# Three emission edits in a graph attention layer: four record loads on another queue, two norms' means emitted later

## The chip, the cores and the metric

The kernel runs on one core of a Trainium2 chip. Its time is the device time of one execution in microseconds (us). The core has five engines that run side by side, each in its own order: PE (TensorE, matrix products; PEld is its weight load), DVE (VectorE), ACT (ScalarE), POOL (GpSimd) and SP (SyncE, here a queue for transfers). An instruction that isn't ready holds up everything behind it on its engine. DMA queues belong to SP, ACT and POOL; row gathers by index are issued by POOL.

## What is computed

One layer of a graph transformer over 4096 nodes of width 512, 8 heads of 64, all in float32:

```python
hs = layer_norm(x);  ht = layer_norm(h_target)
q = (ht @ Wq + bq) / 8;  k = hs @ Wk + bk;  v = hs @ Wv + bv
logits = where(adj != 0, einsum('thd,shd->hts', q, k), -1e30)
ctx    = einsum('hts,shd->thd', softmax(logits), v)
ht     = layer_norm(ht + ctx @ Wo + bo)              # the norm called n2
ff     = gelu(ht @ W1) @ W2                          # 512 -> 2048 -> 512
out    = layernorm(x + ht + ff)                      # the norm called n3
```

`adj` holds few edges in a row (a node has some 17 neighbours, at most 39 here), so the kernel works on lists of neighbours and doesn't form the 4096 x 4096 logits. A dense fallback (`general_path`) stands behind a flag and isn't run on these inputs.

## The kernel before

**Tiles, slots and records.** The 4096 targets are sorted by their number of neighbours and cut into 32 tiles of 128. A tile has as many slots as its largest node has neighbours (11 to 39; 603 slots in all). For each tile there is a record of 29 words a row, with the row's number (`TGT`), its degree, its norm factors and its first 24 neighbours. The tiles come in two parts of 16. Part A's list is sorted first; part B's edges are found and sorted, and its records scattered to HBM (L871), while part A is already in attention. `prefetch` (L989 to L999) loads the record of tile i+2 when the first slots of tile i are requested: for part A on POOL's queue, for part B on SP's (L998). A record has six buffers.

**Attention.** `attention` (L1186) works through 211 steps of up to three slots (S = 3). For each slot POOL gathers 128 rows of 4 KB, key and value of one neighbour, from HBM into a ring of 17 to 20 slots (`gather`, L984); the requests run four or five steps ahead. In each step DVE multiplies the keys by the query (L1242) and sums them to logits (L1247), ACT takes the exponential, DVE and ACT multiply the values (L1203, L1226), DVE adds some slots (L1207), and PE adds the rest up by transposing into PSUM (`cps`, L1214). Each step yields twice to the weaver; one such yield is a half group of slots.

**The end of a tile.** `finish` (L1097) is a generator that `attention` advances once per half group. It normalizes, multiplies by Wo (L1131, L1135), copies to `h` (L1140) and measures it. When a group (one or two tiles; 17 groups) is complete, it computes the norm n2: DVE adds eps (`n_ve`, L680), POOL raises to the power -0.5 (`n_rs`, L687), DVE multiplies that by the negative mean (`n_nm`, L692), ACT applies both to `h` (L1153), and PE transposes `h` into `h2T` (L1162) for the feed-forward.

**Feed-forward.** `feed` (L1332) waits for `h2T`, then alternates W1 products (`pf`, L1347), gelu on ACT (L1350) and W2 products (`po`, L1356). Halfway it gathers the rows of `x` for the residual (`xt`, L1375). It ends with the generator `end` (L1298) for the norm n3, advanced once per block of the next group's feed-forward: sum and square, `n_ve` (L1312), `n_rs` on POOL, `n_nm` (L1317), ACT's scaling (L1320) and the scatter to the output by POOL (L1324). A buffer of `xt` is free for the next gather when that scatter has landed.

**What sets the order.** `_weave` (L400) emits attention, feed-forward and the lists of part B in turn, by costs that the generators yield; attention and feed-forward of a group have the same total cost. The framework then places the emitted instructions on the engines and may change their order on an engine where one is ready earlier by its own estimates. The engines run in the order so fixed.

Of the kernel before, what the change touches and what calls it, by code (L numbers as in the profile page):

```python
# [17 lines left out]
P = 128  # L18
# [360 lines left out]
RW = E0 + RE  # L379
# [64 lines left out]
def adj_resnorm_kernel(  # L444
# [33 lines left out]
    nc = tc.nc  # L478
# [4 lines left out]
    NT = N // P  # L483
# [29 lines left out]
    recs_d = [dram.tile([n * P, RW], I32, name=f"rec{i}") for i, (_, n) in enumerate(PARTS)]  # L513
# [19 lines left out]
    with tc.tile_pool(name="keep", bufs=1) as keep:  # L533
# [17 lines left out]
        with ExitStack() as late:  # L551
# [126 lines left out]
            def shifted(pool, mv, n, name):  # L678
                ve = pool.tile([P, n], F32, name=name + "_ve")
                nc.vector.tensor_scalar_add(ve, mv[:, :, 1], EPS)  # L680
                return ve

            def power(pool, mv, n, name, ve=None):
                if ve is None:
                    ve = shifted(pool, mv, n, name)
                rs = pool.tile([P, n], F32, name=name + "_rs")
                nc.gpsimd.tensor_tensor(rs, ve, mhalf[:, :n], ALU.pow)  # L687
                return rs

            def negmean(pool, mv, rs, n, name):  # L690
                nm = pool.tile([P, n], F32, name=name + "_nm")
                nc.vector.scalar_tensor_tensor(nm, mv[:, :, 0], -1.0, rs, op0=ALU.mult, op1=ALU.mult)  # L692
                return nm

            def stats(pool, src, mv, name):
                st = pool.tile([P, 6], F32, name=name + "_st")
                nc.vector.bn_stats(st, src)
                nc.vector.bn_aggr(mv, st)
# [290 lines left out]
            def prefetch(i):  # L989
                if i >= NT or i in recs:  # L990
                    return
                r0 = TILES[i][0]
                part = 1 if r0 >= PARTS[1][0] * P else 0
                assert part in done
                r0 -= PARTS[part][0] * P
                rec = sp.tile([P, E0 + MAXE], I32, name="rec", bufs=6)

                (nc.sync if part else nc.gpsimd).dma_start(rec[:, :RW], recs_d[part][r0:r0 + P, :])  # L998
                recs[i] = rec  # L999

            def front(i, idle=0):
# [95 lines left out]
            def finish(i, p, cps, group, hs, mv):  # L1097


                rec, tq, cap = recs[i], tqs.pop(i), TILES[i][1]  # L1100

                nc.vector.scalar_tensor_tensor(p[:, :cap, :], rec[:, E0:E0 + cap].unsqueeze(2)
                                               .to_broadcast([P, cap, H]), 0.0, p[:, :cap, :],
                                               op0=ALU.is_gt, op1=ALU.mult)
                nc.vector.tensor_reduce(sums[:, i, :], p[:, :cap, :].rearrange("p j h -> p h j"),
                                        AX.X, ALU.add)
                ri = sp.tile([P, H], F32, name="ri")
                nc.vector.tensor_scalar_max(ri, sums[:, i, :], SUM_LO)
                nc.vector.reciprocal(ri, ri)
                rx = sp.tile([P, KC, P], F32, name="rb", bufs=1)  # L1110
                rxf = rx.rearrange("p c t -> p (c t)")
                nc.scalar.copy(rxf.rearrange("p (h d) -> p h d", h=H),
                               ri.unsqueeze(2).to_broadcast([P, H, HD]))
                yield
                yield
                prx = ps.tile([P, KC, P], F32, name="t", bufs=2)
                for c in range(KC):
                    nc.tensor.transpose(prx[:, c, :], rxf[:, c * P:(c + 1) * P], ident)
                ct = sp.tile([P, KC, P], F32, name="rb", bufs=1)
                nc.scalar.copy(ct, prx)  # L1120
                yield
                yield
                nc.vector.tensor_mul(ct, cps, ct)
                yield
                yield
                yield
                yield
                pa = ps.tile([P, D], F32, name="t", bufs=2)

                for c in range(KC):  # L1130
                    nc.tensor.matmul(pa[:, c * P:(c + 1) * P], tq[:, D + c * P:D + (c + 1) * P],  # L1131
                                     ident, is_transpose=True, start=c == 0, stop=False,
                                     skip_group_check=True)
                for c in range(KC):
                    nc.tensor.matmul(pa, ct[:, c, :], wo[:, c, :], start=False,  # L1135
                                     stop=c == KC - 1, skip_group_check=True)
                turned.add(i)
                yield
                h = sp.tile([P, D], F32, name="h")
                nc.scalar.copy(h, pa)  # L1140
                yield
                stats(sp, h, mv[:, len(hs), :], "n2")
                hs.append(h)
                if len(hs) < len(group):
                    return
                nh = len(hs)
                ve = shifted(sp, mv[:, :nh, :], nh, "n2")
                yield
                rs = power(sp, mv[:, :nh, :], nh, "n2", ve)
                yield  # L1150
                nm = negmean(sp, mv[:, :nh, :], rs, nh, "n2")
                for j, h in enumerate(hs):
                    nc.scalar.activation(h, h, AF.Identity, bias=nm[:, j:j + 1], scale=rs[:, j:j + 1])  # L1153
                yield
                yield
                w = len(hs) * P
                h2T = sp.tile([P, KC, 2 * P], F32, name="h2T")
                for k2 in range(KC // 2):
                    pt = ps.tile([P, 2, 2 * P], F32, name="t", bufs=2)
                    for k in range(2):  # L1160
                        for j, h in enumerate(hs):
                            nc.tensor.transpose(pt[:, k, j * P:(j + 1) * P],  # L1162
                                                h[:, (k2 * 2 + k) * P:(k2 * 2 + k + 1) * P], ident)
                    for k in range(2):
                        kc = k2 * 2 + k
                        nc.scalar.activation(h2T[:, kc, :w], pt[:, k, :w], AF.Identity,  # L1166
                                             bias=b2c[:, kc:kc + 1], scale=s2c[:, kc:kc + 1])
                h2Ts[GROUPS.index(group)] = h2T
# [129 lines left out]
            def end(group, xs, po):  # L1298

                nt = len(group)  # L1300
                sm = sp.tile([P, 2, 2], F32, name="sm3")
                for j in range(nt):
                    nc.vector.scalar_tensor_tensor(xs[j], xs[j], 1.0, po[j], op0=ALU.mult,
                                                   op1=ALU.add, accum_out=sm[:, j, 0:1])
                nc.vector.tensor_scalar_mul(sm[:, :nt, 0], sm[:, :nt, 0], -1.0 / D)
                yield
                for j in range(nt):
                    nc.scalar.activation(po[j], xs[j], AF.Square, bias=sm[:, j, 0:1],
                                         accum_out=sm[:, j, 1:2])
                yield  # L1310
                ve = sp.tile([P, nt], F32, name="n3_ve")
                nc.vector.tensor_scalar(ve, sm[:, :nt, 1], 1.0 / D, EPS, op0=ALU.mult, op1=ALU.add)  # L1312
                yield
                rs = power(sp, None, nt, "n3", ve)
                yield
                nm = sp.tile([P, nt], F32, name="n3_nm")
                nc.vector.tensor_mul(nm, sm[:, :nt, 0], rs)  # L1317
                yield
                for j in range(nt):
                    nc.scalar.activation(xs[j], xs[j], AF.Identity, bias=nm[:, j:j + 1],  # L1320
                                         scale=rs[:, j:j + 1])
                yield
                for j, i in enumerate(group):
                    ins = nc.gpsimd.indirect_dma_start(  # L1324
                        out=out[:, :], out_offset=bass.IndirectOffsetOnAxis(
                            ap=tags[:, i, TGT:TGT + 1], axis=0),
                        in_=xs[j], in_offset=None)

                    tc.declare_no_dep(ins.ins, group="out", reason="other rows")
                    tc.add_to_no_dep_group("out", ins.ins)  # L1330

            def feed(g):  # L1332
# [55 lines left out]
                output(*last)  # L1388
                yield cost
                ends.append(end(group, xs, po))  # L1390
                if g + 1 == len(GROUPS):
                    while ends:
# [124 lines left out]
```

## Time and profile before

| | |
|---|---|
| median of three runs | 1804.25 us (1801.67 to 1813.1) |
| the profiled execution's own time | 1802.71 us |
| its span in the profile | 1800.9 us |
| attention starts, last gather of keys | about 282 us, about 1640 us |
| last scatter to the output | 1783.1 us |
| granted PE clock, mean | 0.964 |

A row of a group or a wait names engine, line and operation, and reads `out<-in`: what is written from what. In the list of waits, `PE cps L1214 <- DVE kv L1207` means that PE stood idle before an instruction of L1214 until an instruction of L1207 on DVE had ended; the numbers are the total, the count and the longest. `issue` is time in which the engine waited for nothing that the profile shows. In a timeline, a row has its start, its duration, the engine and the instruction, and in brackets the idle time before it with what ended it. A row of stretches has its start and end, then for each engine busy time and, in parentheses, the number of instructions, then granted clock, share of DMA time and GB/s.

### The profile page before, as it was taken

How to read it: one execution, taken by the hardware profiler on the slowest of the kernel's cores; microseconds unless marked ns; L12 is line 12 of the kernel's file. 1: busy time of each engine (PE TensorE's matmuls, PEld its weight loads, DVE VectorE, ACT ScalarE, POOL GpSimd, SP SyncE). 2: the span in 40 equal slices, each digit the busy share in tenths (PEclk: the TensorE clock that was granted, in tenths of full speed). 3: DMA queues.
4: the chain of work that ended last, by engine and by line, in shares of the span. 5: the costliest groups of instructions: out<-in, count | busy, mean ns of one | idle time of the engine just before them, and what ended most of it. 6: DMA issues, size and time to landing. Idle time of an engine off the chain costs nothing. (4 is left out here: it accounts for less than half of the span.)

```text
span 1800.9 us, 22314 instructions
## 1 busy us (share of the span) xinstructions
PE 1657.8 (92%) x6746; PEld 1074.4 (60%) x6746; DVE 1434.2 (80%) x2475; ACT 1235.6 (69%) x3129; POOL 1035.2 (57%) x818
## 2 busy tenths in 40 slices
PE   7999995698999999897899989979999999999995
PEld 3444443566666677565566656656666666666663
DVE  6887786889788879988888989789989798998100
ACT  5876663578687967686677877677878587886210
POOL 1000145757555566788777888778777767782100
PEclk9999998799999999998999999989999999999998
DMA  9999978979878787777888888777787767782000
GB/s 350 373 379 361 346 245 306 362 245 317 275 267 284 266 299 256 256 223 221 310 272 267 290 282 270 262 236 259 247 267 245 250 232 235 256 280 95 24 1 26
DMA packets 142058, 460.99 MB, mean 256 GB/s; under 512 B 18548, under 2 KB 23496, under 8 KB 141928
## 3 DMA queue, kind: packets, MB, share of 16 engines
q0 software_dynamic: 96144, 342.27, 56.6%
q1 hardware_dynamic: 37968, 94.12, 14.9%
q10 hardware_dynamic: 7816, 23.08, 3.2%
q8 instruction: 56, 0.92, 0.2%
q14 instruction: 74, 0.61, 0.1%
HBM read 430.61 MB, written 28.79 MB: 255 GB/s over the span
## 5 line engine op out<-in xcount | busy, mean ns | idle before, releaser
L985 POOL DMA_INDIRECT kv<-kvd,rec x603 | 804.5, 1334 | 336.4 <-PE cps L1214 122.5
L1356 PE MATMUL po<-w,gt 128*128 128x512 f32 x1024 | 469.6, 599 | 0.4 <-ACT gt L1350 0.4
L1347 PE MATMUL pf<-h2T,w 128*128 128x256 f32 (+1 forms) x2176 | 467.0, 368 | 0.2 <-ACT h2T L1166 0.2
L1347 PEld LDWEIGHTS pf<-h2T,w 128*128 128x128 f32 x2176 | 389.2, 191 | 68.4 <-issue 23.2
L1226 ACT ACTIVATE kv<-kv,pa 128x64 f32<-128x64 f32 x1520 | 392.1, 337 | 4.8
L1242 DVE TENSOR_TENSOR kv<-kv,tq 128x1536 f32<-128x1536 f32 (+2 forms) x211 | 352.3, 1677 | 48.0 <-DMA kv<-kvd,rec 35.5
L1247 DVE TENSOR_REDUCE lg<-kv 128x24 f32<-128x1536 f32 (+2 forms) x211 | 351.0, 1667 | 0.5
L1214 PE MATMUL cps<-ident,kv 128*128 128x128 f32 x1724 | 241.1, 287 | 76.4 <-DVE kv L1207 38.9
L1356 PEld LDWEIGHTS po<-w,gt 128*128 128x128 f32 x1024 | 189.4, 193 | 191.9 <-issue 189.7
L1214 PEld LDWEIGHTS cps<-ident,kv 128*128 128x128 f32 x1724 | 213.3, 148 | 150.4 <-DVE kv L1207 50.2
L1203 DVE TENSOR_TENSOR kv<-kv,p 128x1024 f32<-128x1024 f32 (+1 forms) x211 | 251.4, 1193 | 10.9 <-ACT p L1251 9.6
L687 POOL TENSOR_TENSOR n_rs<-n_ve,mhalf 128x2 f32<-128x2 f32 (+2 forms) x51 | 51.4, 1007 | 327.5 <-DVE n_ve L680 148.6
L733 ACT ACTIVATE kv<-kv 128x1024 uint8<-128x1024 int32 x128 | 134.4, 1052 | 53.0 <-DMA kv<-in_adj_dram 24.9
L1350 ACT ACT_TABLE_LOAD x108 | 138.6, 1283 | 1.9
L1350 ACT ACTIVATE gt<-pf 128x512 f32<-128x512 f32 x128 | 76.4, 597 | 87.4 <-PE pf L1347 81.8
L947 PE MATMUL pq<-wk,h2T 128*128 128x512 f32 x256 | 121.6, 618 | 4.3 <-ACT kv L949 2.1
L947 PE MATMUL pq<-wv,h2T 128*128 128x512 f32 x256 | 115.6, 594 | 5.8 <-DVE rbc L662 3.2
L1031 PE MATMUL t<-wq,tq 128*128 128x512 f32 x256 | 117.9, 602 | 0.7 <-ACT tq L1024 0.7
L1135 PE MATMUL t<-wo,rb 128*128 128x512 f32 x256 | 115.5, 592 | 0.0
L742 DVE MAX8 cand<-kv 128x8 uint16<-128x171 uint16 (+1 forms) x384 | 108.4, 325 | 6.5 <-remote 3.7
L1251 ACT ACT_TABLE_LOAD x81 | 103.9, 1283 | 1.5
L1207 DVE TENSOR_TENSOR kv<-kv 128x512 f32<-128x512 f32 x144 | 98.2, 682 | 0.2
(163 smaller groups left out, 1501.4 us busy)
## 6 DMA issues: line engine op xcount, KB each, us to landing
kv<-in_adj_dram SPq DMA_DIRECT2D x128, 512.0 KB
kvd<-tq ACTq DMA_DIRECT2D x23, 512.0 KB
kv<-kvd,rec POOLq DMA_INDIRECT x603
kv<-in_L_gnn_h_target_dram SPq DMA_DIRECT2D x32, 256.0 KB
kv<-in_x_dram SPq DMA_DIRECT2D x15, 512.0 KB
kvd<-kv ACTq DMA_DIRECT2D x9, 512.0 KB
w<-in_L_gnn_W_dram SPq DMA_DIRECT2D x4, 1024.0 KB
w<-in_L_gnn_W_dram ACTq DMA_DIRECT2D x4, 1024.0 KB
```

The lines of the kernel that those rows point to most:

```text
L733: nc.scalar.activation(sg, a, AF.Sign, accum_out=dpart[:, i, h:h + 1])
L947: nc.tensor.matmul(pkv, hT[:, kc, j * P:(j + 1) * P], w[:, kc, :], start=kc == 0, stop=kc == KC - 1)
L985: issues[:] = [nc.gpsimd.indirect_dma_start(out=dst, out_offset=None, in_=table[:, :], in_offset=bass.IndirectOffsetOnAxis(ap=idx, axis=0) ...
L1031: nc.tensor.matmul(pq, hT[:, kc, :], wq[:, kc, :], start=kc == 0, stop=kc == KC - 1)
L1203: nc.vector.tensor_tensor(v4, v4, p[:, j0:j0 + m, :].unsqueeze(3) .to_broadcast([P, m, H, HD]), ALU.mult)
L1214: nc.tensor.matmul(cps[:, c, :], kv[:, j, D + c * P:D + (c + 1) * P], ident, is_transpose=True, start=j0 + j == 0 and c == 0, stop=j0 + n ...
L1226: newest[:] = [nc.scalar.mul(v, v, pa[:, hd:hd + 1]).ins]
L1242: nc.vector.tensor_tensor(kv[:, :n, :D], kv[:, :n, :D], tq[:, :D].unsqueeze(1).to_broadcast([P, n, D]), ALU.mult)
L1247: logits[:] = [nc.vector.tensor_reduce(lg[:, :n, :], kv[:, :n, :D].rearrange("p j (h d) -> p j h d", h=H), AX.X, ALU.add).ins]
L1347: nc.tensor.matmul(pf[:, k, :], w1[(f0 + k) // KC][:, kc, (f0 + k) % KC * P:((f0 + k) % KC + 1) * P], h2T[:, kc, :w], start=kc == 0, stop= ...
L1350: nc.scalar.activation(gt, pf, AF.Gelu_apprx_tanh)
L1356: nc.tensor.matmul(po[j], gt[:, k, j * P:(j + 1) * P], w2[(f0 + k) // KC][:, (f0 + k) % KC, :], start=False, stop=f0 + k == FC - 1, skip_g ...
```

## The change

Three places. `prefetch` loads the records of the last four tiles (28 to 31, in part B) through POOL's queue instead of SP's. In `finish`, four yields instead of one stand between the power and the product with the mean of n2, so that `n_nm` and the two instructions after it are emitted three half groups later. In `end`, two yields instead of one stand between the power and the product with the mean of n3.

```diff
@@ prefetch
-                (nc.sync if part else nc.gpsimd).dma_start(rec[:, :RW], recs_d[part][r0:r0 + P, :])
+                (nc.sync if part and i < NT - 4 else nc.gpsimd).dma_start(rec[:, :RW], recs_d[part][r0:r0 + P, :])
@@ finish
                 rs = power(sp, mv[:, :nh, :], nh, "n2", ve)
-                yield
+                for _ in range(4):
+                    yield
                 nm = negmean(sp, mv[:, :nh, :], rs, nh, "n2")
@@ end
                 rs = power(sp, None, nt, "n3", ve)
                 yield
+                yield
                 nm = sp.tile([P, nt], F32, name="n3_nm")
```

The first two lines added shift what follows in `finish` by one line, and the third by one more.

## The prediction

> **What bounds the kernel now.** I read the busy shares, then stretches of the span, then the waits of the worst stretch, then its timeline. Columns of the stretches: start:end, length, busy time of each engine with its instructions in parentheses, granted clock, DMA share, GB/s.
>
> ```profile
> PE 1657.8 (92%) x6746; PEld 1074.4 (60%) x6746; DVE 1434.2 (80%) x2475; ACT 1235.6 (69%) x3129; POOL 1035.2 (57%) x818
> ```
> ```profile
> 300.00:420.00 120.00, 88.06 (x464) 65.50 (x464) 101.21 (x133) 72.91 (x227) 81.34 (x67) 0.87 0.87 315
> 420.00:800.00 380.00, 371.99 (x1694) 258.99 (x1694) 331.51 (x544) 298.83 (x764) 243.80 (x198) 1.00 0.80 270
> 800.00:1200.00 400.00, 357.01 (x1499) 240.53 (x1498) 348.50 (x381) 291.45 (x807) 315.91 (x234) 0.93 0.81 269
> 1200.00:1640.00 440.00, 435.47 (x1810) 291.22 (x1809) 390.73 (x450) 336.90 (x875) 323.72 (x234) 1.00 0.75 247
> 1640.00:1784.00 144.00, 139.03 (x582) 93.01 (x581) 33.04 (x94) 43.27 (x96) 14.39 (x16) 1.00 0.08 24
> ```
>
> PE is the bound almost everywhere: its work is fixed, so the end moves only with PE's idle time and with what its clock loses after idling. PE is idle 31.9 us in 300:420, 8.0 in 420:800, **43.0 in 800:1200**, 4.5 in 1200:1640, 5.0 in the tail. In 1200:1640 and in the tail, an earlier norm buys next to nothing. In 800:1200 are the groups with most slots (42 to 51). DVE is idle there 51.5 us; POOL is busy 315.9 of 400 us, and of its 84.1 idle us some 52 are the 0.30 us it takes before almost every instruction, so it has about 32 us, 5.8 of which are waits of the residual's gather. The waits of that stretch:
>
> ```profile
> PE cps L1214 <- DVE kv L1207: 33.8, 10, 11.0
> DVE n_nm L692 <- POOL n_rs L687: 25.5, 3, 14.1
> PE t L1162 <- ACT h L1153: 6.3, 1, 6.3
> POOL xt L985 <- DMA out_dram<-xt,tags: 5.8, 4, 2.7
> DVE n_nm L692 <- issue: 5.4, 1, 5.4
> DVE n_nm L1317 <- POOL n_rs L687: 3.5, 2, 2.9
> ```
>
> DVE waits 25.5 + 5.4 = 30.9 us for n2's power: 5.39 before group 6's product with the mean, 4.85 in group 7, 6.59 in group 8, 14.08 in group 9. The timeline of group 8 shows how (other rows left out):
>
> ```profile
> 1056.45 3.45 POOL L985 DMA_INDIRECT kv<-kvd,rec  x1 [0.30 <-issue]
> 1060.20 0.94 POOL L985 DMA_INDIRECT kv<-kvd,rec  x1 [0.30 <-issue]
> ...
> 1063.94 0.94 POOL L985 DMA_INDIRECT kv<-kvd,rec  x1 [0.30 <-issue]
> 1064.91 0.72 POOL L687 TENSOR_TENSOR n_rs<-n_ve,mhalf 128x2 f32<-128x2 f32 x1
> 1065.67 0.16 DVE L692 SCALAR_TENSOR_TENSOR n_nm<-mv,n_rs 128x2 f32<-128x2 f32 x1 [6.59 <-POOL n_rs L687]
> 1065.86 1.52 ACT L1153 ACTIVATE h<-h,n_nm,n_rs 128x512 f32<-128x512 f32 x2 [7.78 <-DVE n_nm L692]
> 1066.73 0.69 PE L1162 MATMUL t<-ident,h 128*128 128x128 f32 x2 [6.28 <-ACT h L1153]
> ```
>
> The power isn't slow (0.72 us). It stands on POOL behind gathers at 1.24 us each, while DVE is blocked in front of the next logits, ACT behind DVE, PE behind ACT.
>
> **Part 1, n2's mean.** I counted slots of attention ahead of these instructions in the two built programs. The emission moves three half groups, but the framework undoes most of it. POOL's power of groups 6, 7, 8, 9 stands after slots 246, 298, 349, 400 now, and after 247, 298, 349, 400 in the changed program. DVE's product moves by one step of logits in groups 7 and 8 (also 0, 1, 2 and 5), in 6 and 9 only behind one values product, and not at all against the slots in 10 to 14. A step of logits is 1.68 + 1.67 = 3.35 us (rows L1242, L1247), a values product with its addition 1.19 + 0.68 = 1.87. So the waits become 5.39 + 1.24 - 1.87 = 4.8, 4.85 - 3.35 = 1.5, 6.59 - 3.35 = 3.2, 14.08 - 1.87 = 12.2: 9.2 us less. Behind the waiting product on DVE stand the next step's logits and values, for which ACT and PE wait. Groups 10 to 13 wait 2.85, 7.15, 10.77 and 4.54 us now and will still; PE hides them behind feed-forward.
>
> **Part 2, n3's mean.** Its product waits 12.6 us in all, only 3.5 of it in 800:1200 (2.92 and 0.61). The product moves nearer to its power (from 8 slots short of it to 6, and from 9 to none), which saves 2 x 1.24 = 2.5 of the one and all of the other: 3.1 us.
>
> How much reaches PE: its gaps that follow n2's waits are 3.03 us (at 968), 6.28 (at 1066), and 8.46 + 1.47 + 2.12 (1177 to 1194), none after group 6: 21.4 of 30.9, or 0.69. So 12.3 x 0.69 = 8.5 us. After a gap PE runs at half speed for a while (8 transposes of L1214 take 1.97 us at 1177 and 1.04 at 1164); one long gap less gives back some 2 us. **Gain: 10.5 us.**
>
> **Part 3, what moves with them on POOL.** With n3 later, the output's scatter comes later, and the gather of the next residual rows, which needs its buffer, now stands 0 to 2 key gathers behind it from group 4 on; before, mostly 3 to 12. From a scatter's start to such a gather's takes 6.25 us (1163.45 to 1169.70) or 5.9 (956.70 to 962.63), 3.06 in the quiet tail. Scatter and two gathers fill 3 x 1.24 to 1.64, so each such gather stops POOL some 1.8 us. Eight of them in this stretch make 14.4 in place of 5.8: +8.6 us. Also, gathers issued while DVE waits take 0.94 us, and the stretch's mean is 1.35 (260.1 us over 193): without the 24 or so in the waits it is 1.41. Nine or so gathers that no longer fall into a wait cost 0.47 each: +4.2. That is 12.8 us more of POOL, of the 26 it has free. Bounds 0 and 12.8; I take +5, nearer the middle, as the ring's lead hides part.
>
> A rule speaks against the change here. The Trainium skill, "SBUF — State Buffer", section "Who interferes with whom", says that VectorE and GpSimd share one pair of ports under an exclusive lock: one of them blocks for the other's whole instruction. Were every two-input VectorE instruction such a lock, all that VectorE gains would be lost to POOL, and Part 1 would sum to nothing; the 1.41 against 0.94 us here is a third of that, for reasons that no row shows.
>
> **Part 4, the feed-forward's lag.** Group 0's `h` is transposed one step of slots later, and the first W1 products begin behind 132 of the 1724 values transposes instead of 120. From group 1 on, feed-forward stands 14 to 18 us of PE time further back at the same slot (W1 pairs at 0.45 us, W2 at 0.86, counted in both orders). PE's total stays; the lag costs only where PE then starves. Bounds: 0, if attention fills the time (420:800 has 48.5 us of idle DVE, and POOL waits 70.0 us for PE there), and 16. One more step without feed-forward at the start is one more gap of about 5 us (4.87, 5.49, 5.94 and 5.12 lie at 296, 320, 330 and 349), and part of a gap at 416 (5.55) is filled by the first group's late W2. I take **+4**. In the tail PE has 16 us more to do but no new gap.
>
> **Part 5, the four records.** SP loses four loads of 0.32 us and nothing waits for it. POOL gets four of 0.596 (row L998) + 0.30 = 3.6 us, past slot 450, among key gathers. That is 1200:1640, where POOL waits 29.3 us for PE and 17.8 for DVE to free the ring; the cover hides them, and without it they cost 3.6. The buffer of a record is that of six tiles before, long done. I take 0.
>
> **Sum** on the profiled execution's own time of 1802.71 (0.1% under the median of 1804.25): -10.5 + 5 + 4 = -1.5, **1801 us**. Own range 1790 to 1812.
>
> **Rivals.** *Slower: POOL's stops take the place of DVE's.* Each residual gather right behind its scatter stops POOL, and every later power comes later by as much, so n2's waits stay as long as they are. Place: 800:1200 first, decided when POOL's new stops there pass the 26 us it has free, which happens if landing takes longer than 6 us. Then Parts 1 and 2 give 0, Part 3 its full 12.8, Part 4 its 4. In 1200:1640 the eight gathers of groups 9 to 12 cost up to 13.6 where now none waits, and in groups 11 to 13 the power stands behind a scatter that waits for ACT (1.5 us a time now, 7.6 over 5): up to 6 more. Half of these 19.6 shows: 12.8 + 4 + 10 = +27, 1829. For it: POOL is full there but for 26 us. Against: the ring holds five steps of lead.
>
> *Faster: the waits vanish.* If POOL's lead at the power is a few slots larger than I count, all of 30.9 + 3.5 goes: 34.4 x 0.69 = 23.7, three gaps' slow clock 6, Part 4 at 2, Part 3 at 0: -28, 1775. For it: the waits are a few gathers each, and group 8's gap has PE one step later. Against: group 9's, the longest, barely moves.
>
> *The wait only changes its name.* DVE reaches the next logits sooner and waits there for the gathers (5.7 us now), since POOL sets the pace; also the case in which the edits do nothing. 1804, range 1800 to 1810.
>
> **Chances.** Forecast 0.36, faster rival 0.25 (1762 to 1788), slower 0.31 (1814 to 1845), renamed wait 0.08. Leaving out the fastest third of the faster and the upper third of the slower gives 1770 to 1832. One per cent is 18 us, about what a measurement of this kernel can tell from no change. Nearly all of the faster rival and 0.02 of the forecast lie beyond it below: 0.26; nine tenths of the slower above: 0.28; within: 0.46.
>
> **What the profile after would show.** Part 1: groups 7 and 8 with waits of 1 to 3 us before L692, group 9 still above 10; PE's gap near 1066 gone. Part 2: no wait before n3's product in 800:1200. Part 3: waits of the residual's gather for the output at 14 us in that stretch, and its key gathers above 1.35 us. Part 4: the last key gather earlier than 1640 and a longer PE-only tail. I am wrong if POOL's waits for the output exceed 26 us, if group 9's wait vanishes, or if PE shows new gaps in 1200:1640.

## The result: slower by 1%

Measured beside each other on one chip, the changed kernel takes 1822.93 us (median of 6 runs, 1820.46 to 1824.79) and the kernel before 1806.15 us: a ratio of **1.0095, 95% interval 1.0074 to 1.0116**, some 17 us more. The forecast was 1801 us, a change of -1.5 us. Its own range of 1790 to 1812 did not hold the time; the range with the rivals, 1770 to 1832, did, some 8 us farther from its upper end by luck, since the records' edit, priced at nothing, gained that much. The mechanism of the forecast did not hold. The profiled execution of the changed kernel took 1824.5 us with a span of 1822.8 us.

The busy shares, then the same stretches as before (start:end, length, busy time of each engine with its instructions, granted clock, DMA share, GB/s); the tail now reaches 1805:

```profile
PE 1666.6 (91%) x6746; PEld 1078.6 (59%) x6746; DVE 1434.8 (79%) x2475; ACT 1224.3 (67%) x3121; POOL 1072.9 (59%) x822
```
```profile
300.00:420.00 120.00, 90.92 (x478) 67.66 (x477) 107.68 (x144) 76.93 (x237) 87.61 (x70) 0.86 0.90 330
420.00:800.00 380.00, 360.79 (x1623) 248.65 (x1622) 328.76 (x542) 290.88 (x750) 252.38 (x199) 0.98 0.78 267
800.00:1200.00 400.00, 353.91 (x1508) 241.30 (x1507) 343.66 (x368) 287.72 (x792) 320.41 (x222) 0.94 0.76 256
1200.00:1640.00 440.00, 421.38 (x1726) 280.24 (x1725) 375.00 (x434) 321.18 (x848) 332.61 (x237) 0.98 0.74 247
1640.00:1805.00 165.00, 165.00 (x694) 112.27 (x693) 47.26 (x106) 51.99 (x123) 20.07 (x20) 1.00 0.11 38
```

PE's idle time went from 31.9 to 29.1 us in 300:420, **from 8.0 to 19.2** in 420:800, from 43.0 to 46.1 in 800:1200 and **from 4.5 to 18.6** in 1200:1640: 87.5 before, 113.0 after. So the loss lies in the two stretches where PE had next to no idle time, and the stretch in which the gain was expected got none. PE's last product starts at 1810.9 us instead of 1778.4, 32.4 us later: 25.5 us are that idle time, and the other 6.9 are PE busy longer with the same work, beside a granted clock of 0.98 instead of 1.00 in the same two stretches. That the span grew by 21.9 us only is due to the program's last 10 us, below.

The waits of 800:1200 (total, count, longest):

```profile
PE cps L1215 <- DVE kv L1208: 36.9, 10, 8.9
DVE kv L1243 <- DMA kv<-kvd,rec: 23.1, 5, 7.8
DVE xt L1304 <- DMA xt<-in_x_dram,tags: 14.9, 2, 9.2
POOL xt L985 <- DMA out_dram<-xt,tags: 9.1, 4, 3.2
DVE n_nm L692 <- POOL n_rs L687: 8.5, 2, 6.1
DVE n_nm L692 <- issue: 3.0, 1, 3.0
```

The waits before n2's product fell from 30.9 to 11.5 us (8.5 + 3.0), by more than forecast. Others stand in their place: for key gathers 23.1 us where it was 5.7, and 14.9 us, new, for the rows of the residual. PE's wait for DVE is 36.9 us; it was 33.8.

### The profile page after: what moved, and what is told of

It is laid out like the page before. It is cut to its first block, busy times and chain, and to the rows that moved or that the text cites. A ratio compares the mean times of both kernels' runs of the same rounds, so it can differ in the third digit from the quotient of the medians.

```text
span 1822.8 us, 22282 instructions
## 1 busy us (share of the span) xinstructions
PE 1666.6 (91%) x6746; PEld 1078.6 (59%) x6746; DVE 1434.8 (79%) x2475; ACT 1224.3 (67%) x3121; POOL 1072.9 (59%) x822
## 5 line engine op out<-in xcount | busy, mean ns | idle before, releaser
L985 POOL DMA_INDIRECT kv<-kvd,rec x603 | 844.1, 1400 | 307.5 <-issue 132.3
L1349 PE MATMUL pf<-h2T,w 128*128 128x256 f32 (+1 forms) x2176 | 473.8, 372 | 1.4 <-ACT kv L1227 0.9
L1349 PEld LDWEIGHTS pf<-h2T,w 128*128 128x128 f32 x2176 | 394.2, 194 | 68.6 <-issue 20.8
L1243 DVE TENSOR_TENSOR kv<-kv,tq 128x1536 f32<-128x1536 f32 (+2 forms) x211 | 352.6, 1678 | 70.2 <-DMA kv<-kvd,rec 53.5
L1031 PE MATMUL t<-wq,tq 128*128 128x512 f32 x256 | 121.6, 618 | 8.4 <-ACT tq L1024 6.9
L1252 ACT ACTIVATE p<-lg 128x24 f32<-128x24 f32 (+2 forms) x179 | 39.1, 218 | 99.8 <-DVE lg L1248 79.4
```

The lines of the kernel that those rows point to most:

```text
L985: issues[:] = [nc.gpsimd.indirect_dma_start(out=dst, out_offset=None, in_=table[:, :], in_offset=bass.IndirectOffsetOnAxis(ap=idx, axis=0) ...
L1031: nc.tensor.matmul(pq, hT[:, kc, :], wq[:, kc, :], start=kc == 0, stop=kc == KC - 1)
L1243: nc.vector.tensor_tensor(kv[:, :n, :D], kv[:, :n, :D], tq[:, :D].unsqueeze(1).to_broadcast([P, n, D]), ALU.mult)
L1349: nc.tensor.matmul(pf[:, k, :], w1[(f0 + k) // KC][:, kc, (f0 + k) % KC * P:((f0 + k) % KC + 1) * P], h2T[:, kc, :w], start=kc == 0, stop= ...
```

## The experiments

Each ratio stands against the kernel before, measured beside it on the same chip, with its 95% interval; 0.001 is 1.8 us.

### One edit at a time

The diff of each is the part of the change that its expectation names: n2's four yields, n3's second yield, the records on GpSimd's queue, and both norms without the records.

> Only n2's product with the mean is emitted three half groups later. Theory A (the residual's gather comes too late): in the changed kernel DVE waits 14.9 us in 800:1200 before L1304 for the rows of x, since n3's later emission puts the output's scatter and with it that gather later. Without n3's edit the gathers stand 3 to 8 slots earlier against their reader, so these waits shrink to under 5 us and the time is 8 to 12 us under the changed kernel: 1811 to 1815, ratio to before about 1.004. Theory B (the feed-forward's lag of 14 to 18 us of PE time, which this edit alone makes): PE's new idle time in 420:800 (+11 us) and 1200:1640 (+14 us) stays and the ratio is 1.007 to 1.010.

> Only n3's product with the mean is emitted one step later. The feed-forward doesn't lag here; the residual's gather of groups 6 and 7 stands 13 and 6 slots later than before (one slot behind its reader in group 6). Theory A: DVE waits 5 to 10 us before L1304 around 1020 to 1130, ratio 1.003 to 1.006. Theory B: ratio 0.998 to 1.002.

> Only the records of the last four tiles go through POOL's queue. Both theories: hidden, POOL gets some 3.6 us past slot 450, ratio 0.999 to 1.001; a rival that POOL is the bound there gives +3.6 us, 1.002.

> Both norms' edits without the records'. Both theories: the changed kernel's time, ratio 1.0095 within 0.002, with DVE's wait of about 15 us before L1304. If the records matter, it is 3 us or more faster than the changed kernel.

| edit | ratio |
|---|---|
| n2 alone | 1.0113 (1.0063 to 1.0163) |
| n3 alone | 0.9996 (0.9978 to 1.0013) |
| records alone | 0.9956 (0.9938 to 0.9975) |
| n2 and n3 | 1.0113 (1.0067 to 1.0158) |

n2's edit alone costs some 20 us, n3's nothing that shows. The records' edit, which the forecast had priced at nothing and its own expectations at 0 to 3.6 us of loss, **gains 8 us**. So two questions: what in n2's edit costs 20 us, and what the records have to do with the time.

### n2: the lag and the later products apart

In the order of PE's instructions, the lag of feed-forward comes from group 1 alone: with four yields in group 1 and one elsewhere it is 13 to 18 us of PE time, as with four everywhere; with four from group 6 on it is 0. That separates the two effects.

```diff
 # f_g1                                      (f_late: GROUPS.index(group) >= 6)
-                yield
+                for _ in range(4 if group is GROUPS[1] else 1):
+                    yield
 # f_g1late
+                for _ in range(4 if GROUPS.index(group) == 1 or GROUPS.index(group) >= 6 else 1):
 # f_y3: range(3)      f_not01: range(1 if GROUPS.index(group) < 2 else 4)
 # f_lead2, after the ACT scaling of h
-                yield
-                yield
```

> Four yields before n2's product only in group 1, one in every other group; records and n3 as before. In the order this alone puts feed-forward back by the same 13 to 18 us of PE time, from group 2 to the end, as the edit in all groups does (with the edit in all groups but group 1 it does not), while the products of the groups after it stand where the shifted feed-forward puts them. Theory 'lag' (late feed-forward finds no idle PE to fill and ends as a longer tail): 1818 to 1826, ratio 1.009 to 1.013, the tail of PE some 15 us longer than before's. Rival 'position' (the later products of groups 6 to 9, and what they shift on POOL, cost the time): 1800 to 1807, since those groups have the old number of yields.

> Four yields before n2's product from group 6 on, one in groups 0 to 5; records and n3 as before. In the order feed-forward stands where it stood before (0 us of lag up to the last group), and the products of groups 7 and 8 stand one step of logits later, as in the full edit. Theory 'lag': no loss of 20 us, and the gain that was forecast for the mean of n2 can be seen: 1790 to 1802, ratio 0.993 to 1.000. Rival 'position': 1815 to 1825, nearly all of the loss of the full edit.

> Four yields before n2's product in group 1 and from group 6 on, one in groups 0 and 2 to 5; records and n3 as before. It joins the two halves that were run alone: group 1 alone (feed-forward 13 to 18 us of PE time later; 1.006 of before) and groups 6 to 16 alone (no lag; 0.999). Theory 'interplay' (the later products of the late groups cost only where feed-forward lags, since then the residual's gathers and the products meet on POOL): 1820 to 1828, ratio 1.010 to 1.014, as the edit in all groups. Rival 'sum' (the two halves simply add up, and the rest of the full edit's loss comes from groups 2 to 5): 1805 to 1813, ratio 1.003 to 1.008.

> Three yields before n2's product in all groups instead of four; records and n3 as before. In the order feed-forward is 4 to 7 us of PE time later than before instead of 14 to 18. Theory 'lag': the loss falls with the lag, to a third or a half of the full edit's 20 us: 1805 to 1814, ratio 1.003 to 1.008. Rival 'any shift of the products costs': 1818 to 1826, as with four.

> Four yields before n2's product in all groups but 0 and 1; records and n3 as before. Feed-forward is 0 to 4 us of PE time later. Theory 'lag': no loss worth the name, 1798 to 1806, ratio 0.998 to 1.004, although 15 of 17 products have the full shift. Rival 'position': above 1815, since all groups from 2 on are shifted as in the full edit.

> The opposite sign: one yield before n2's product as before, but the two yields between ACT's scaling and the transposes of h left out, so feed-forward stands 4 to 7 us of PE time further ahead than before. Theory 'lag', if it works in both directions: 1796 to 1800, ratio 0.996 to 0.999, the tail shorter by 4 to 7 us. If before already fills all of PE's idle time, the earlier transposes only wait for ACT: 1802 to 1810.

| kernel | lag, us of PE time | products later in | ratio |
|---|---|---|---|
| f_late | 0 | groups 6 to 16 | 0.9991 (0.9968 to 1.0015) |
| f_g1 | 13 to 18 | group 1 | 1.0060 (1.0040 to 1.0081) |
| f_g1late | 14 to 18 | groups 1, 6 to 16 | **1.0146** (1.0116 to 1.0177) |
| f_y3 | 4 to 7 | all, three yields | 1.0040 (1.0026 to 1.0055) |
| f_not01 | 0 to 4 | groups 2 to 16 | 1.0053 (1.0029 to 1.0076) |
| f_lead2 | -4 to -7 | none | 1.0046 (1.0021 to 1.0070) |

*f_late* answers for Part 1: without the lag, the same shift of the late groups is worth nothing. These are its waits in 800:1200:

```profile
PE cps L1215 <- DVE kv L1208: 38.6, 10, 12.1
DVE n_nm L692 <- POOL n_rs L687: 20.5, 4, 9.9
DVE kv L1243 <- DMA kv<-kvd,rec: 15.7, 5, 6.7
DVE kv L1243 <- issue: 6.4, 2, 4.4
```

n2's waits fell by 10.4 us, from 30.9 to 20.5, close to the 9.2 of the forecast. The waits before the key product L1243 rose by 12.9, from 5.7 + 3.5 to 15.7 + 6.4, and PE's idle time from 43.0 to 45.1. The wait changed its name: DVE reaches the next keys sooner and waits there for gathers. The new waits stand behind n2's products of groups 6 and 7 (at 859 and 962): 2.0 and 2.6 us at 878 and 882, 2.8 and 6.7 at 966 and 985. The last of them reaches PE:

```profile
985.10 1.76 DVE L1243 TENSOR_TENSOR kv<-kv,tq 128x1536 f32<-128x1536 f32 x1 [6.68 <-DMA kv<-kvd,rec]
991.97 1.97 PE L1215 MATMUL cps<-ident,kv 128*128 128x128 f32 x8 [5.14 <-DVE kv L1208]
```

PE's gaps of 6.28 and 8.46 us at 1066 and 1177 did shrink, to 1.74 and 3.14; those of 4.03 and 3.03 at 882 and 968 grew to 7.57 and 7.22, and the one at 992 is new. PE's 2 us of idle time more are within what one order gives: d_1 and e_rec, which have the order of before here, have 43.5 and 47.7 us.

*f_g1* shows the lag at work with next to none of the rest. PE's idle time in 420:800 rises from 8.0 to 18.0 us, in 1200:1640 from 4.5 to 11.1, and falls from 43.0 to 32.2 in 800:1200:

```profile
420.00:800.00 380.00, 361.98 (x1635) 250.71 (x1634) 331.46 (x536) 289.60 (x753) 253.74 (x200) 0.98 0.79 272
800.00:1200.00 400.00, 367.81 (x1578) 243.39 (x1577) 357.35 (x393) 295.32 (x816) 322.81 (x232) 0.98 0.81 267
1200.00:1640.00 440.00, 428.92 (x1778) 286.65 (x1777) 389.18 (x448) 331.41 (x873) 332.04 (x231) 0.99 0.75 247
```

The last key product starts 9 us earlier than before (1642 for 1651), the last W2 product 6 us later (1784 for 1778). Attention wins back part of the PE time that it got early, not all, and the rest is a longer tail. That was Part 4's mechanism, at +11 us (7 to 15) instead of +4. The time lies between the two expectations; the tail grew by the 15 us that 'lag' said.

*f_g1late* decides between sum and interplay. The halves are worth +11 and -2 us; together they cost **+26** (21 to 32). 'Sum' (3 to 8 thousandths) is out. *f_y3* fits a loss that falls with the lag. *f_not01* and *f_lead2* do not: some 8 to 10 us at almost no lag, or with feed-forward earlier. f_not01 has the shift of f_late and that of groups 2 to 5 beside it; what makes its loss was not looked for. The lag is therefore not a price per microsecond; the order before does better than its neighbours on either side, for reasons that these two runs don't single out.

### What carries the interplay

With feed-forward late, the output's scatters come late too, and the next gathers of residual rows stand right behind them on POOL. This is POOL in f_g1late (rows of a timeline: start, duration, engine, instruction, idle time before it and what ended it; key gathers left out):

```profile
872.90 2.27 POOL L1325 DMA_INDIRECT out_dram<-xt,tags  x1 [0.31 <-ACT pa L1224]
...
879.34 2.57 POOL L985 DMA_INDIRECT xt<-in_x_dram,tags  x1 [1.67 <-DMA out_dram<-xt,tags]
...
883.46 4.17 POOL L1325 DMA_INDIRECT out_dram<-xt,tags  x1 [0.30 <-issue]
887.94 0.97 POOL L985 DMA_INDIRECT gid<-rest_d,rec  x1 [0.30 <-issue]
...
890.46 0.95 POOL L985 DMA_INDIRECT xt<-in_x_dram,tags  x1 [0.30 <-issue]
```

and the next wait of DVE:

```profile
896.93 1.76 DVE L1243 TENSOR_TENSOR kv<-kv,tq 128x1536 f32<-128x1536 f32 x1 [5.61 <-DMA kv<-kvd,rec]
```

In the 18.8 us from 872.9 to 891.7, two scatters, two residual gathers, one stop of 1.67 us and another gather leave room for four key gathers, where POOL issues one in 1.25 us when nothing holds it up. DVE waits 5.61 us for keys, and 3.48 more at 907; PE has other products until 911.6 and then waits for DVE:

```profile
907.26 1.76 DVE L1243 TENSOR_TENSOR kv<-kv,tq 128x1536 f32<-128x1536 f32 x1 [3.48 <-DMA kv<-kvd,rec]
914.79 1.09 PE L1215 MATMUL cps<-ident,kv 128*128 128x128 f32 x8 [3.23 <-DVE kv L1208]
```

POOL's stops of this kind in 800:1640 (total, count, longest), in f_g1 and in f_g1late:

```profile
POOL xt L985 <- DMA out_dram<-xt,tags: 3.1, 3, 1.3
```
```profile
POOL xt L985 <- DMA out_dram<-xt,tags: 9.2, 6, 3.0
```

Before and f_late have 5.8, the changed kernel 14.1. In that stretch, 12 of the 18 residual gathers of f_g1late stand 0 to 2 key gathers behind a scatter, and 12 in f_g1 too, where the kernel before has 4; so that place in the order comes with the lag, and the longer stops with the late groups' shift. To test it, the residual's rows are loaded by SP's queue, so that POOL has neither gathers nor stops. These three kernels leave the sorted targets' index out: they add other rows of `x` than the layer asks for:

```diff
-                            with behind(issues):
-                                gather(xt, x, tags[:, i, TGT:TGT + 1])
+                            nc.sync.dma_start(xt, x[i * P:(i + 1) * P, :])
```

> The kernel before, with the residual's rows loaded in their order by SP's queue and not gathered by GpSimd; so the 32 rows tiles added to the result are other rows than the reference's. GpSimd has 32 gathers less (about 40 us with their starts) and none of its waits for the output's scatter (5.8 us in 800:1200). If GpSimd sets the pace in 800:1200, PE's idle time there falls from 43 to some 30 us and the time to 1780 to 1795; if the order of the rest decides, 1795 to 1806. GpSimd's closing instructions, with 717 transfers: 1.8 + 6.8 us if they grow with each transfer within a ring of some 107 (749 would be its last place, 750 its first), about 0.4 + 0.7 to 1.0 if 749 is an unlucky number.

> The same loads by SP's queue, with four yields before n2's product in group 1 and from group 6 on (1.0146 of before with the gathers on GpSimd, +26 us); it also adds other rows than the reference's. Theory 'residual': the interplay lies in the residual's gathers standing right behind the scatters on GpSimd, so against x_b only the lag's cost is left: +7 to +14 us. Rival 'keys': it lies in the key gathers and the ring alone: +20 to +30 us against x_b.

> The residual's rows in their order by SP's queue (other rows than the reference's), four yields before n2's product in group 1 only. x_b, without a shift, ran at 0.990 of before, x_g1late, with the late groups shifted too, at 1.000. If what is left there is the lag: 0.996 to 1.001, 12 to 18 us above x_b. If the late groups' products still cost on their own: 0.990 to 0.995, at most 9 us above x_b.

| residual's rows | no shift | lag alone | lag and late groups |
|---|---|---|---|
| gathered by POOL | 1 | 1.0060 | 1.0146 |
| loaded by SP | 0.9899 (0.9859 to 0.9938) | 0.9990 (0.9963 to 1.0017) | 0.9999 (0.9977 to 1.0021) |

With POOL relieved, the late groups' shift adds 0.9 thousandths to the lag, where it adds 8.6 with the gathers on POOL (each within some 3.5). The lag costs about the same in both rows (6.0, and 9.1 within some 5). So most of the 15 us of interplay needs the residual's gathers on POOL; the intervals leave room for up to 8 us of it without them. x_g1late alone, 18 us above x_b, lay between its two expectations; x_g1 decides. (Of the 18 us that x_b gains, 3.3 lie in the end of the program, see below; x_g1 and x_g1late have them too.) The runs don't separate the stops themselves from POOL being 32 gathers fuller; the timeline above shows both at once. x_g1 and x_g1late scatter widely (1782 to 1807 and 1789 to 1807 us), so only their medians are used.

The reverse was tried on the kernel before, with the one extra transfer of the next section:

```diff
-                    if f0 == FC // 2:
+                    if f0 == (FC * 5 // 8 if nt == 2 else FC // 2):
```

> The kernel before with the last record by GpSimd's queue (0.995 of before by itself) and the residual's rows gathered one block of feed-forward later, where the gathers of groups 3 to 7 stand 8 to 19 key gathers behind a scatter instead of 0 to 12, except one group with 0 to 3. If the gathers' stops behind the scatters cost time in the kernel before as well: 1780 to 1792, ratio 0.988 to 0.994. If they are hidden there: 1790 to 1796, ratio 0.994 to 0.997. If the rows now come too late for their reader in some groups (4 to 10 slots ahead of it): above 1796.

0.9962 (0.9941 to 0.9983): what the extra transfer gives alone (d_1, 0.9951). In the order of before, moving the gathers gains nothing that shows, within some 5 us.

### The records: the end of the program

The gain of the records' edit lies behind the last computation. After the last scatter, GpSimd runs two closing instructions that the profile's busy shares don't count. Their durations in the traces, by the number of transfers that the program issues on GpSimd (e_n2, e_n3, e_n2n3 and the f_ kernels have those of before):

```
transfers   kernel           INC_SWDGE_SEM   DRAIN
717         x_b                 1.815         6.688
741         d_m8                2.295         8.648
749         before              2.455         9.302
750         d_1                 0.360         0.727
753         e_rec, d_x4, after  0.420         0.972
757         d_8                 0.500         1.298
```

```diff
 # d_1 (d_8: NT - 8; d_x4: a second load of each of the last four records, by gpsimd;
 #           d_m8: nc.sync if part or i >= NT // 2 - 8)
-                (nc.sync if part else nc.gpsimd).dma_start(rec[:, :RW], ...)
+                (nc.sync if part and i < NT - 1 else nc.gpsimd).dma_start(rec[:, :RW], ...)
```

> All records by SP's queue as before, and beside them the last four records once more through GpSimd's queue into four spare tiles, so GpSimd issues 753 transfers as in the changed kernel and SP keeps its own. If the closing instructions of GpSimd (2.46 + 9.30 us at the end of before, 0.42 + 0.97 in the kernel with the records' edit alone) go by what GpSimd's queue carried: they fall to 0.4 + 1.0 us here too, and the time to about 1794. If they go by SP's transfers: 2.5 + 9.3 us stay, and the time is 1800 to 1806.

> Only the last record (tile 31) by GpSimd's queue: 750 transfers there instead of 749. If any change in the number of GpSimd's transfers sets its closing instructions right (place within a ring): 0.4 + 1.0 us and about 1794. If a threshold lies at 752 or 753: 2.5 + 9.3 us as before, 1800 to 1806. If it falls evenly with the count: a quarter of the gain, closing instructions of about 9 us in all.

> The last eight records by GpSimd's queue: 757 transfers. If the closing instructions grow with each transfer within a ring (750: 0.36 + 0.727; 753: 0.42 + 0.972; so 0.02 and 0.082 us for each): 0.50 + 1.30 us. If every number but 749 gives the small values: 0.4 + 1.0.

> The records of tiles 8 to 15 by SP's queue instead of GpSimd's: 741 transfers. Ring: eight places before 749, so 2.3 + 8.65 us. Unlucky number: 0.4 + 1.0 us or less.

d_x4 leaves SP's loads alone, adds four on GpSimd and gives 0.9960 (0.9938 to 0.9981): the count on GpSimd's queue decides, not SP's. d_1 gets it all with one transfer: **0.9951 (0.9934 to 0.9968)**, which rules out a threshold at 752 and an even fall. d_8 and d_m8 (single runs, read for these two rows) match to 0.01 us what their expectations took from a ring, x_b to 0.11: in these rows each transfer adds 0.020 and 0.0817 us, and between 749 and 750 the pair falls back by 10.7 us, or 105 transfers' worth. The kernel before happened to stop on the last count ahead of that fall. Why the pair takes time by this count, no run shows.

So d_1 and e_rec, one line each, beat both kernels: 1793.4 and 1793.6 us.

## Why the prediction was wrong, point by point

**Part 1** (-8.5 us with Part 2, and -2 for the clock). Groups 7 and 8 came close to the count: they kept 0 and 2.4 us (forecast 1.5 and 3.2), and PE's gap of 6.28 us at 1066 became one of 1.53. Group 6 rose to 6.07 (forecast 4.8), and group 9, forecast at 12.2, came down to 2.96, near the sign of being wrong that the forecast had named for it:

```profile
1074.95 0.16 DVE L692 SCALAR_TENSOR_TENSOR n_nm<-mv,n_rs 128x2 f32<-128x2 f32 x1 [2.42 <-POOL n_rs L687]
1076.02 0.44 PE L1163 MATMUL t<-ident,h 128*128 128x128 f32 x2 [1.53 <-ACT h L1154]
1178.48 0.16 DVE L692 SCALAR_TENSOR_TENSOR n_nm<-mv,n_rs 128x2 f32<-128x2 f32 x1 [2.96 <-issue]
```

The step that failed is the next one, "0.69 of it reaches PE": f_late, with 10.4 us less of n2's wait, has no less idle PE (45.1 us after 43.0) and no gain (0.9991). That share was read off the gaps that followed the waits; but POOL was busy or starting an instruction in all but 32 of these 400 us, so a wait for POOL that goes comes back at the next instruction that needs POOL. The rival "the wait only changes its name", at 0.08, was right for this part.

**Part 2** (-3.1 us before n3's product). n3's product has no wait left in 800:1200, as forecast; e_n3 as a whole is worth nothing (0.9996); that the way to PE is missing here too is likely, and not shown by a run of its own.

**Part 3** (+5 of 0 to 12.8). POOL's stops behind the output were to be 14 us in 800:1200 and are 9.1, four of 2.3 us and not eight of 1.8; key gathers were to be above 1.35 us and are 1.44. The mechanism was there, but the forecast priced it on POOL alone and as a term of its own. It shows only together with the lag: in f_late the stops stay at 5.8 us in 800:1640 and nothing is lost; in f_g1late, against f_g1, they rise from 3.1 to 9.2 and the time by 15 us. The two waits of 9.16 and 5.71 us for the residual's rows, for which the forecast has no term at all, come with n3's edit on top of n2's (e_n2 and e_n3 alone don't have them): in the order, the second tile's gather went from 5 and 12 slots ahead of its reader to 10 and 5 behind it, in groups 6 and 7. They stand out in the list and cost nothing more that shows, since e_n2, without them, loses as much as e_n2n3 (within some 12 us).

**Part 4** (+4 of 0 to 16). This is the term that was mis-sized: the lag alone costs 11 us (f_g1), and with the late groups' shift beside it 26. The forecast held that attention would mostly fill the time; in 420:800 it could not, since PE then stood in order before work that ACT had not delivered. The changed kernel's waits of PE in that stretch:

```profile
PE t L1163 <- ACT tq L1024: 5.7, 1, 5.7
PE t L1031 <- ACT tq L1024: 5.7, 1, 5.7
PE cps L1215 <- DVE kv L1208: 2.5, 1, 2.5
```

Before, the longest was 3.1. f_g1, with the lag alone, has two such gaps there as well, both behind copies of ACT:

```profile
587.77 1.11 PE L1118 MATMUL t<-ident,rb 128*128 128x128 f32 x4 [4.36 <-ACT h2T L1167]
798.10 5.98 PE L1031 MATMUL t<-wq,tq 128*128 128x512 f32 x8 [7.12 <-ACT tq L1024]
```

The forecast also put the lag's origin in group 0; it is group 1, since f_g1's first W1 product stands behind 120 transposes, as before, and f_g1 has the whole lag. "New gaps in 1200:1640" was a sign of being wrong that the forecast named, and they are there: 5.44 us at 1457, 3.92 at 1538, 3.72 at 1281.

**Part 5** (0). The loads themselves cost nothing, as said. The end of the program was not in the forecast at all: -10.4 us in the traces, a gain by luck. Without the records the change stands at 1.0113 (e_n2n3); less the 0.0044 of e_rec that is 1.0069, where 1.0095 was measured: the intervals allow it, and what may lie between stays open.

**The rivals.** "Slower: POOL's stops take the place of DVE's", 1829 us, came nearest in time and named the right queue, but the wrong course: n2's waits did go, POOL's stops stayed far under the 26 us from which it was to decide, and its first place, 800:1200, holds only 3.1 of the 25.5 us that PE lost. "Faster" had the waits go further than the forecast did, as they did, and failed with it at the way to PE. The longer PE-only tail came; the last key gather came later (1654 us), not earlier than 1640.

## What to carry to other kernels

A wait for an engine that is itself nearly full is not by itself a gain to be had: count what that engine delivers next, and expect the wait there. A yield before a consumer also delays everything that sleeps until that consumer has run, and one group's late start can shift a whole stream to the end; so look first at which group sets that offset. Extra yields in the other groups cost less here (nothing that shows in f_late, some 10 us in f_not01), and in no run did they gain anything. Two shifts that cost little alone can cost more than their sum where they meet on one queue: weigh them together before adding terms.

## What the hardware showed that I had not expected

**GpSimd's closing instructions cost 1.1 to 11.8 us**, by the number of transfers that the program issued on that queue: they grow by 0.10 us a transfer, and fall back between 749 and 750. How many transfers a period has in general, these runs don't show beyond the 105 steps of that fall.

**A key gather's time depends on what DVE executes when it starts.** In 800:1200 of the kernel before, by the trace: 49 that start during the key product L1242 take 1.80 us on average and 39 during the values product L1203 1.72 (both of them two-input products), 63 during the reduction L1247 0.95, 25 while DVE is idle 0.95. In the changed kernel the four are 2.18, 2.14, 0.94 and 0.94. So the prediction's "a third of that, for reasons that no row shows" has its reason: a gather that meets a long two-input product takes about twice as long, and the reduction, which lasts as long as the key product, holds none up. The other 16 are too few to read (4 that start during the short additions of L1207 take 1.32). The Trainium skill, "SBUF — State Buffer", section "Who interferes with whom", says it that way: an instruction of VectorE with two SBUF inputs contends with a GpSimd instruction that reads SBUF, and a reduction on trn2 never does. These means agree; the prediction had set the rule against a mean over all of DVE's work.
